# A two-layer graph network in float32: conv 2's node product in three float32r passes, b2 added by an accumulating transfer, and a new order of the work

## The chip, the cores and the metric

The kernel runs on one core of a Trainium2 chip. Its time is device time in microseconds (us), from the median of several runs; the runs shown for the kernel before are three. One execution of each kernel was also recorded by the hardware profiler, and its instructions are read below. The engines are named as in the profile: PE is TensorE (matmuls), PEld its weight loads, DVE is VectorE, ACT is ScalarE, POOL is GpSimd, and SP issues most of the transfers.

## The reference, cut to what matters

Each of 128 graphs g has 128 nodes with 512 features, x[g], and an adjacency matrix adj[g] of 128 x 128. All is float32.

```
h  = relu(layernorm(x))                        # over the 512 features
H  = (adj != 0);  w = adj[0, :]                # per graph
Be = 1 / columnsum(H);  Dn = 1 / (H w)
conv(z, W, b) = Dn * (H (Be * (H^T (z W^T)))) + b
h1 = layernorm(relu(conv(h, W1, b1))) * gamma + beta    # 1024 wide
x  = x + conv(h1, W2, b2) + h                           # back to 512
h2 = relu(layernorm(x))
agg = (adj h2) / max(rowsum(adj), 1e-6)
out = x + relu([h2, agg] W^T)
```

H Be H^T is one symmetric 128 x 128 matrix per graph, the node matrix S. Conv 1 applies S to the 512 features before W1; conv 2 applies W2 first (1024 to 512) and then S to the result: that last product is conv 2's node product.

## The kernel before

**Stages.** One graph is one unit of work: its 128 nodes lie on the 128 partitions. The function step(s) writes out by hand one pass of a software pipeline in which several graphs are in different stages: conv 1 of graph s, the normalisation and conv 2 of s-1, the node product of conv 2 and the first half of layer 1 of s-2, the weights and aggregation of layer 1 of s-3, the end of s-4, and preparations for s+1, s+2 and s+3. A stage is a small function with an argument g, decorated so that it runs once and only for graphs that exist. head() does graphs 0 to 2 together with the loading and splitting of the weights; tail() does the last graphs. The instructions of each engine run strictly in the order in which these functions emit them, and so do the transfers on each issuing queue (SP, ACT, POOL). The framework adds the waits between engines. No planner runs: the order in the source is the order on the chip.

**Exact products.** The large matmuls (lines 455 and 460) are made with float32r operands, which TensorE takes in one pass. To keep float32's accuracy each operand is split in two or three parts. ACT makes a high part (L537, L426), DVE or POOL subtracts it from the value for a low part (the helper combine, L80, or L430), and DVE makes a third combination of both (L546, L433). product() then runs three groups of matmuls: high by high and low by low into one bank of PSUM (names ending in m: rm, gm, bm, am) and the third into a second bank (rd, gd, bd, ad). ACT copies the first bank out with a factor just over one, and DVE adds the second. Only the small products are left as plain float32 matmuls: ps_s (the node matrix, L375), pz (conv 1's node product, L413) and py (conv 2's node product, L628).

**Around the change.** conv2_weights runs gm and gd; conv2_main (ACT, L615) and conv2_weights_out (DVE, L619) make G; conv2_bias adds c0, the share of beta, on POOL (L80, tile g); conv2_nodes multiplies S by G in float32 into py; conv2_out (DVE, L632) adds py times Dn to X. X itself was prepared by residual, in which POOL adds h and then b2 (broadcast to all partitions, b2_bc) to x. layer1_self_main and layer1_self_out (L704, L716) bring the last product out of PSUM, and finish (L721) applies relu, adds X and issues the store on SP. Small work sits on DVE: scales (L305, L306) turns a variance into the two numbers of a layernorm; mean_operator (L320 to L323) divides adj by its row sums; incidence (L361 to L369) makes H and H Be; node_scale (L386 to L389) makes Dn. inner_turn and layer1_turn (L516) are block transposes; their operands come through DRAM and back (n_scratch, h_scratch, an_scratch, L501 and L509).

**Buffers.** The main products rotate through six banks of PSUM, the small ones (ps_s, pz, py) through two. Many SBUF tiles share a tag and so a buffer: a tile can be written only when all readers of the one before it are done. In the last graphs, place() puts tiles into weight buffers that are no longer needed. fill(n) puts dummy matmuls of n columns ahead of the next bank.

Of the kernel before, what the change touches and what calls it, by code (L numbers as in the profile page):

```python
# [24 lines left out]
def gnn_kernel(  # L25
# [45 lines left out]
    pool = ctx.enter_context(tc.tile_pool(name="pool", bufs=1))  # L71
    dram = ctx.enter_context(tc.tile_pool(name="dram", bufs=3, space=DRAM))
# [9 lines left out]


# [118 lines left out]
    def unit():  # L202
        t = pool.tile([P, 3, P], FP, tag="anp", name="unit").bitcast(FR)
        zero = pool.tile([P, P], FP, tag="ant", name="zero")
        nc.gpsimd.memset(zero, 0.0)
        for i, v in enumerate((1.0, -1.0)):
            nc.gpsimd.affine_select(out=t[:, i], in_=zero, compare_op=ALU.not_equal, fill=v, base=0,
                                    pattern=[[-1, P]], channel_multiplier=1)
            UNIT.append(t[:, i])
# [49 lines left out]
    def beta_out():  # L259
        nc.vector.tensor_scalar(c0, BETA[0], DOWN_12, None, MUL)  # L260
# [28 lines left out]

    STATS = {}  # L290

    def sums(key, src, junk, width, func=AF.Identity):
        STATS[key] = t = pool.tile([P, 8], FP, tag=f"st{key[0]}", name="st", bufs=2)
# [9 lines left out]
    def scales(g, kind):  # L303
        t = STATS[kind, g]
        nc.vector.reciprocal(t[:, 4:5], t[:, 3:4])  # L305
        nc.vector.tensor_tensor(t[:, 5:6], t[:, 1:2], t[:, 4:5], MUL)  # L306
# [9 lines left out]
    def mean_operator(g):  # L316

        a = ADJ.pop(g)
        deg = pool.tile([P, 1], FP, tag="deg", name="deg", bufs=2)
# [3 lines left out]
        nc.vector.tensor_scalar(a, a, deg, None, MUL)  # L323
# [13 lines left out]
    def mean_transpose(g):  # L337
# [4 lines left out]
        parts = place(pool, [P, 3, P], "anp", "anp", g).bitcast(FR)  # L342
# [14 lines left out]
    def incidence(g):  # L357
# [4 lines left out]
        SB[g] = sb = pool.tile([P, P + 1], FP, tag="sb", name="sb")  # L362
        nc.vector.tensor_scalar(sb[:, P : P + 1], at[:, 0:1], DOWN_12, None, MUL)
        cnt = pool.tile([P, 1], FP, tag="cnt", name="cnt", bufs=3)
# [4 lines left out]
        nc.vector.tensor_scalar(sb[:, :P], at, cnt, None, MUL)  # L369
# [3 lines left out]
    def node_matrix(g):  # L373
        ps = small_bank("ps_s")
        nc.tensor.matmul(ps[:, : P + 1], HT.pop(g), SB.pop(g), start=True, stop=True)  # L375
        s = pool.tile([P, P + 1], FP, tag="s", name="s", bufs=4)
        copy(s, ps[:, : P + 1], AF.Copy)  # L377
# [4 lines left out]
    def node_scale(g):  # L382
        w = DN[g]
        DN[g] = dn = pool.tile([P, 3], FP, tag="dinv", name="dinv", bufs=6)
# [4 lines left out]
        nc.vector.tensor_scalar(dn[:, 1:2], dn[:, 0:1], ONE_UP, None, MUL)  # L389

# [14 lines left out]
    def residual(g, eng=nc.gpsimd):  # L405
        combine(eng, X[g], X[g], H0[g], ADD)
        combine(eng, X[g], X[g], b2_bc, ADD)
# [205 lines left out]
    def conv2_main(g):  # L613
        G[g] = t = place(pool, [P, D], "A", "g", g)
        copy(t, PY.pop(g), AF.Copy, scale=ONE_UP)  # L615

    @stage
    def conv2_weights_out(g):
        nc.vector.tensor_tensor(G[g], PG.pop(g), G[g], ADD)  # L619
# [4 lines left out]

    @stage
    def conv2_nodes(g):
        PY[g] = py = small_bank("py")
        nc.tensor.matmul(py, S.pop(g), G.pop(g), start=True, stop=True)  # L628

    @stage  # L630
    def conv2_out(g):
        nc.vector.scalar_tensor_tensor(X[g], PY.pop(g), DN.pop(g)[:, 0:1], X[g], MUL, ADD)  # L632
# [86 lines left out]
    def finish(g):  # L719
        o = OP.pop(g)[0]  # L720
        nc.vector.scalar_tensor_tensor(o, o, 0.0, X.pop(g), MAX, ADD)  # L721
        nc.sync.dma_start(out=out[g], in_=o)

    def step(s):
        layer1_self_main(s - 4)
        conv2_bias(s - 2)
        layer1_high(s - 3)  # L730
        x_norm(s + 1)
        node_matrix(s + 1)
        conv2_nodes(s - 2)
        layer1_self_out(s - 4)
        mean_out(s - 3)
        inner_out(s - 1)
        inner_in(s - 1)
        finish(s - 4)
        layer1_low(s - 3)
        load_x(s + 2)  # L740
        mean_in(s - 3)
        load_adjb(s + 3)
        conv1_main(s, 0)
        conv2_out(s - 2)
        conv1_nodes(s + 1)
        conv1_weights(s, 1)
        load_adj(s - 2)
        layer1_sums(s - 2)
        layer1_spread(s - 2)
        layer1_rest(s - 3)  # L750
        conv1_out(s, 0)
        conv1_main(s, 1)
        layer1_mean(s - 3)
        inner_turn(s - 1)
        scales(s - 2, 3)
        layer1_self(s - 3)
        conv1_high(s + 1)
        conv1_out(s, 1)
        residual(s + 1)
        inner_high(s - 1)  # L760
        layer1_norm(s - 2)
        layer1_mean_main(s - 3)
        conv1_low(s + 1)
        conv1_bias(s, 0)
        mean_transpose(s - 3)
        conv1_bias(s, 1)
        inner_low(s - 1)
        layer1_mean_out(s - 3)
        layer1_trip_out(s - 2)
        inner_sums(s)  # L770
        layer1_mean_high(s - 3)
        conv1_rest(s + 1)
        mean_operator(s - 2)
        node_scale(s + 1)
        inner_spread(s)
        scales(s, 2)
        inner_rest(s - 1)
        conv2_weights(s - 1)
        layer1_mean_low(s - 3)
        mean_rest(s - 3)  # L780
        layer1_mean_rest(s - 3)
        incidence(s + 2)
        aggregate(s - 3)
        conv1_weights(s + 1, 0)
        x_sums(s + 2)
        inner_norm(s)
        x_spread(s + 2)
        conv2_main(s - 1)
        layer1_trip_in(s - 2)
        conv2_weights_out(s - 1)  # L790
        layer1_turn(s - 2)
        scales(s + 2, 1)

    def head():
        load_adjb(0, nc.scalar)
        load_w1(0, 0)
        copy(eps_root, eps, AF.Sqrt)
        w1[0].high(0)
        load_x(0)
        load_w1(0, 1)  # L800
        w1[0].low(0)
        x_sums(0)
        x_spread(0)
        load_w1(1, 0)
        fill(2816)
        w1[0].high(1)
        scales(0, 1)
        load_x(1)
        incidence(0)
        w1[0].low(1)  # L810
        unit()
        load_adjb(1)
        x_norm(0)
        w1[0].rest(0, nc.vector)
        node_matrix(0)
        conv1_nodes(0)
        load_w1(1, 1)
        incidence(1)
        x_sums(1, "A")
        load_w2(0)  # L820
        w1[1].high(0)
        load_affine()
        x_spread(1)
        scales(1, 1)
        conv1_high(0)
        node_matrix(1)
        conv1_low(0)
        conv1_rest(0)
        w1[1].high(1)
        w1[1].low(0)  # L830
        w1[0].rest(1, nc.gpsimd)
# [481 lines left out]
```

## Time and profile before

| what | value |
|---|---|
| median of 3 runs | 2480.91 us (2480.42 to 2481.21) |
| the profiled execution | 2481.01 us, span 2478.9 us from its first to its last instruction |
| granted TensorE clock, mean over the span | 0.998 |
| busy PE / PEld / DVE / ACT / POOL | 2461.9 / 2005.7 / 2004.5 / 1940.0 / 1715.1 us |
| 0 to 75 us | PE busy 67.7, DVE 63.3, ACT 63.6, POOL 47.0 |
| 100 to 2419 us | PE busy 2319.0, DVE 1876.1, ACT 1824.6, POOL 1643.5 of 2319.0 |
| 2419 to 2479 us | PE busy 52.1, DVE 46.2, ACT 31.9, POOL 5.6 |

A line of a timeline has the start in us from the beginning of the span, the duration in us, the engine, the source line, the operation, the tile written and the tiles read, the shape, and how many like it are merged; in brackets stands the engine's idle time ahead of it and what ended it. A group line has total busy us and the mean ns of one. A line of waits has the total, the number and the longest in us. Records of one engine overlap: an instruction often starts before the record of the one ahead of it ends, so what an instruction costs on a busy engine is the distance from its start to the next start.

### The profile page before, as it was taken

To read this page: it belongs to the slowest core of one execution; us is meant where nothing else is said; L and a number is where in the kernel's file an instruction comes from. 1 tells how busy PE (TensorE), PEld (TensorE's weight loads), DVE (VectorE), ACT (ScalarE), POOL (GpSimd) and SP (SyncE) were. 2 spreads that over 40 slices of the span, in tenths; PEclk is the share of its full clock that TensorE was granted. 3 is DMA by queue.
4 is the path that set the end of the run, shared out by engine and by line. 5 is a ranking of instruction groups with operands and counts; after the bars stand their busy time and mean duration, and the time that the engine had idled before them with its cause. 6 is when DMAs were issued, how large, how long until landed. Compare 5 with 4: busy or idle time off the path is not lost.

```text
span 2478.9 us, 41066 instructions
## 1 busy us (share of the span) xinstructions
PE 2461.9 (99%) x11188; PEld 2005.7 (81%) x11188; DVE 2004.5 (81%) x4906; ACT 1940.0 (78%) x4125; POOL 1715.1 (69%) x2275
## 2 busy tenths in 40 slices
PE   8999999999999999999999999999999999999998
PEld 6788888888888888888888888888888888888886
DVE  8888888888878888888788888787888888888887
ACT  8878877787788778877887787778777877887775
POOL 6677767776777677767767776777677767776761
PEclk9999999999999999999999999999999999999999
DMA  7344344434443443344334433443444344334432
GB/s 186 120 129 122 119 129 126 125 120 129 130 123 119 129 132 122 117 131 129 122 121 130 128 122 124 129 126 121 129 127 123 121 129 129 121 120 129 132 112 93
DMA packets 408951, 311.35 MB, mean 126 GB/s; under 512 B 176656, under 2 KB 339984, under 8 KB 408720
## 3 DMA queue, kind: packets, MB, share of 16 engines
q1 hardware_dynamic: 407888, 308.66, 40.6%
q8 instruction: 88, 1.44, 0.3%
q14 instruction: 143, 1.17, 0.2%
q10 hardware_dynamic: 576, 0.07, 0.0%
q0 software_dynamic: 256, 0.01, 0.0%
HBM read 166.21 MB, written 142.34 MB: 124 GB/s over the span
## 4 chain that ended last, share of the span: by engine, by line
PE 97%; DVE 1%; ACT 1%; DMA 0%; issue 0%; ACTq 0%; POOL 0%; SPq 0%; DVEq 0%
PE rm L455 19%; PE gm L455 19%; PE gd L460 9%; PE am L455 9%; PE bm L455 9%; PE rd L460 9%; PE bd L460 5%; PE ad L460 5%; PE py L628 4%; PE pz L413 4%; PE am L710 2%; PE ad L710 1%; PE ps_s L375 1%; DMA adjb<-in_adj_dram 0%; ACT r L294 0%
## 5 line engine op out<-in xcount | busy, mean ns | idle before, releaser
L80 POOL TENSOR_TENSOR g<-g,c 128x256 f32<-128x256 f32 x246 | 178.2, 745 | 631.9 <-DVE g L619 631.9
L80 POOL TENSOR_TENSOR r<-r,b_bc 128x256 f32<-128x256 f32 x500 | 360.2, 739 | 53.0 <-DVE r L480 47.4
L80 POOL TENSOR_TENSOR nl<-nt,nh 128x256 fp32r<-128x256 f32 x488 | 345.4, 734 | 0.0
L80 POOL TENSOR_TENSOR x_t<-x_t,b_bc 128x256 f32<-128x256 f32 x256 | 240.9, 961 | 3.0 <-DMA b_bc<-in_b_dram 3.0
L80 POOL TENSOR_TENSOR hl<-ht,hh 128x256 fp32r<-128x256 f32 x248 | 231.2, 954 | 6.4 <-ACT hh L537 6.2
L704 ACT ACTIVATE o<-am 128x512 f32<-128x512 f32 x127 | 76.1, 599 | 203.4 <-PE am L710 203.4
L294 ACT ACTIVATE h<-x_t 128x512 f32<-128x512 f32 x255 | 159.1, 624 | 96.6 <-DVE x_t L632 96.5
L480 DVE SCALAR_TENSOR_TENSOR r<-rd,dinv,r 128x512 f32<-128x512 f32 x256 | 190.6, 744 | 20.1 <-PE rd L460 7.3
L310 ACT ACTIVATE h<-x_t,st 128x512 f32<-128x512 f32 x255 | 204.7, 803 | 0.0
L683 DVE TENSOR_TENSOR gb_t<-bd,gb_t 128x512 f32<-128x512 f32 x127 | 87.9, 692 | 137.2 <-ACT gb_t L679 134.5
L80 POOL TENSOR_TENSOR x_t<-x_t,h 128x256 f32<-128x256 f32 x256 | 185.6, 744 | 5.6 <-ACT h L310 5.5
L632 DVE SCALAR_TENSOR_TENSOR x_t<-py,dinv,x_t 128x512 f32<-128x512 f32 x128 | 96.1, 751 | 115.3 <-PE py L628 115.3
L299 ACT ACTIVATE h<-x_t,st 128x512 f32<-128x512 f32 x255 | 182.7, 717 | 4.2
L413 PEld LDWEIGHTS pz<-s,h 128*128 128x128 f32 x1024 | 134.6, 192 | 60.1 <-ACT s L377 41.9
L475 ACT ACTIVATE r<-rm,dinv 128x512 f32<-128x512 f32 x256 | 173.2, 677 | 12.0 <-PE rm L455 11.7
L80 POOL TENSOR_TENSOR bl<-gb_t,bh 128x256 fp32r<-128x256 f32 x246 | 177.2, 739 | 1.8 <-PE am L455 1.8
L619 DVE TENSOR_TENSOR g<-gd,g 128x512 f32<-128x512 f32 x127 | 87.8, 692 | 92.3 <-PE gd L460 89.8
L310 ACT ACTIVATE r<-r,st 128x1024 f32<-128x1024 f32 x128 | 157.6, 1231 | 1.2 <-DVE st L306 1.2
L516 DVE STREAM_TRANSPOSE nt<-nb 128x1024 f32<-128x1024 f32 x127 | 156.3, 1230 | 1.6 <-DMA nb<-n_scratch 0.8
L721 DVE SCALAR_TENSOR_TENSOR o<-o,x_t 128x512 f32<-128x512 f32 x127 | 152.1, 1198 | 4.2
L546 DVE SCALAR_TENSOR_TENSOR nd<-nh,nl 128x1024 fp32r<-128x1024 f32 x127 | 155.2, 1222 | 0.0
L455 PE MATMUL rm<-w11h,z 128*128 128x512 f32 x512 | 151.3, 417 | 0.0
(217 smaller groups left out, 7242.3 us busy)
## 6 DMA issues: line engine op xcount, KB each, us to landing
n_scratch<-r SPq DMA_DIRECT2D x128, 512.0 KB, 2.6
nb<-n_scratch SPq DMA_DIRECT2D x508, 128.0 KB, 2.8
x_t<-in_x_dram SPq DMA_DIRECT2D x128, 256.0 KB, 2.9
h_scratch<-h SPq DMA_DIRECT2D x127, 256.0 KB, 2.0
hb<-h_scratch SPq DMA_DIRECT2D x508, 64.0 KB, 2.0
out_dram<-o SPq DMA_DIRECT2D x127, 256.0 KB, 2.2
adj_t<-in_adj_dram SPq DMA_DIRECT2D x128, 64.0 KB, 1.9
an_scratch<-adj_t SPq DMA_DIRECT2D x128, 64.0 KB, 1.7
```

The source lines that it names most:

```text
L80: eng.tensor_tensor(dst[:, s], a[:, s], b[:, s], op)
L294: copy(junk, src, func, accum_out=t[:, 0:1])
L299: copy(junk, src, AF.Square, bias=t[:, 1:2], accum_out=t[:, 2:3])
L310: copy(dst, src, func, bias=t[:, 5:6], scale=t[:, 4:5])
L413: nc.tensor.matmul(z[:, k * P : (k + 1) * P], H0[g][:, k * P : (k + 1) * P], S[g], start=True, stop=True)
L455: nc.tensor.matmul(pm, left[i](k), right(i, k), start=(i == 0 and k == 0), stop=(i == 1 and k == kk - 1))
L460: nc.tensor.matmul(pd, left[2](k), right(2, k), start=(k == 0), stop=(k == kk - 1), skip_group_check=True)
L475: copy(R[g][:, HALVES[half]], PY.pop((g, half)), AF.Copy, scale=DN[g][:, 1:2])
L480: nc.vector.scalar_tensor_tensor(r, PR.pop((g, half)), dn[:, 0:1], r, MUL, ADD)
L516: nc.vector.transpose(nt.rearrange("p k (i b) -> p k i b", b=B), t.rearrange("p i k a -> p k i a"))
L546: nc.vector.scalar_tensor_tensor(t, h, 2.0**-12, low, MUL, SUB)
L721: nc.vector.scalar_tensor_tensor(o, o, 0.0, X.pop(g), MAX, ADD)
```

## The change

Groups 3 to 120 are called steady; for them

- conv 2's node product becomes three float32r matmuls. S (now scaled by 4096) is split in three by node_high (ACT) and node_rest (two DVE operations), G in three by conv2_high (ACT), conv2_low (DVE) and conv2_rest (DVE). Two matmuls go to a bank ym, one to yd, both from the six main banks; conv2_out becomes two DVE operations, one for each bank.
- residual adds b2 by a transfer from b2_bc into X that accumulates, issued on POOL.
- finish leaves the store to a stage of its own, store, later on SP's queue.

For all groups

- conv2_main and conv2_weights_out carry a factor 4096 into G.
- scales keeps the reciprocal alone; the product goes to a stage shifts, on POOL or ACT or DVE as each call says. mean_operator leaves its scaling to mean_scale (ACT in the step), and incidence its last scaling to incidence_scale (POOL in the step).
- In the step, layer1_low, inner_low and layer1_mean_low go from POOL to DVE.
- Some tiles move to other pools (small, left).
- step, head and tail have a new order; head's fill of 2,816 columns becomes two of 128, and the tail gets one of 512.

Its core, with the whole new step (of head and tail, whose order changes throughout, the start of head):

```diff
+    FIRST, LAST = 3, N - 8
+
+    def steady(g):
+        return FIRST <= g <= LAST
+
+    def moved(t, src):
+        nc.gpsimd.dma_start(out=t, in_=src, accum_op=ADD)
...
+    def scaled(eng, dst, src, c):
+        if eng is nc.scalar:
+            copy(dst, src, AF.Copy, scale=c)
+        else:
+            eng.tensor_scalar(dst, src, c, None, MUL)
...
-        nc.vector.tensor_tensor(t[:, 5:6], t[:, 1:2], t[:, 4:5], MUL)
+
+    @stage
+    def shifts(g, kind, eng):
+        t = STATS[kind, g]
+        scaled(eng, t[:, 5:6], t[:, 1:2], t[:, 4:5])
...
-        nc.vector.tensor_scalar(a, a, deg, None, MUL)
+        ADJ[g] = a, deg
+
+    @stage
+    def mean_scale(g, eng):
+        a, deg = ADJ[g]
+        scaled(eng, a, a, deg)
...
-        nc.vector.tensor_scalar(sb[:, :P], at, cnt, None, MUL)
+        SB[g] = sb, cnt
+
+    @stage
+    def incidence_scale(g, eng):
+        SB[g], cnt = SB[g]
+        scaled(eng, SB[g][:, :P], HT[g], cnt)
...
-        copy(s, ps[:, : P + 1], AF.Copy)
+        copy(s, ps[:, : P + 1], AF.Copy, scale=4096.0 if steady(g) else 1.0)
...
-        combine(eng, X[g], X[g], b2_bc, ADD)
+        if steady(g):
+            moved(X[g], b2_bc)
+        else:
+            combine(eng, X[g], X[g], b2_bc, ADD)
...
+    @stage
+    def conv2_high(g):
+        if steady(g):
+            GP[g] = t = left.tile([P, 2, D], FP, tag="t3", name="gp").bitcast(FR)
+            copy(t[:, 0], G[g], AF.Copy, scale=DOWN)
+
+    @stage
+    def conv2_low(g, eng=nc.gpsimd):
+        if steady(g):
+            combine(eng, GP[g][:, 1], G.pop(g), GP[g][:, 0], SUB)
+
+    @stage
+    def node_high(g):
+        if steady(g):
+            SP[g] = t = left.tile([P, 8, P], FP, tag="t1", name="sp").bitcast(FR)
+            copy(t[:, 0], S[g], AF.Copy, scale=DOWN / 4096.0)
+
+    @stage
+    def node_rest(g):
+        if steady(g):
+            t, full = SP[g], S.pop(g)
+            nc.vector.scalar_tensor_tensor(t[:, 1], t[:, 0], -4096.0, full, MUL, ADD)
+            nc.vector.scalar_tensor_tensor(t[:, 2], t[:, 0], -4097.0, full, MUL, ADD)
+
+    @stage
+    def conv2_rest(g):
+        if steady(g):
+            t = SP[g].rearrange("p k c -> p (k c)")[:, D : 2 * D]
+            h, l = GP[g][:, 0], GP[g][:, 1]
+            nc.vector.scalar_tensor_tensor(t, h, DOWN_12, l, MUL, SUB)
+            GP[g] = h, l, t
...
+        pm, pd = bank("ym"), bank("yd")
+        parts, (h, l, d) = SP.pop(g), GP.pop(g)
+        nc.tensor.matmul(pm, parts[:, 0], h, start=True, stop=False)
+        nc.tensor.matmul(pm, parts[:, 1], l, start=False, stop=True)
+        nc.tensor.matmul(pd, parts[:, 2], d, start=True, stop=True)
+        PY[g] = pm, pd
...
+        for p, c in zip(PY.pop(g), (1, 0)):
+            nc.vector.scalar_tensor_tensor(X[g], p, dn[:, c : c + 1], X[g], MUL, ADD)
...
     def step(s):
+        node_high(s - 2)
+        layer1_high(s - 3)
         conv2_bias(s - 2)
+        inner_out(s - 1)
+        inner_in(s - 1)
+        conv2_high(s - 2)
+        node_rest(s - 2)
+        node_matrix(s + 1)
+        mean_out(s - 3)
+        layer1_low(s - 3, nc.vector)
+        layer1_self_main(s - 4)
+        conv1_weights(s, 1)
+        mean_in(s - 3)
+        conv2_low(s - 2, nc.vector)
+        layer1_self_out(s - 4)
+        conv2_rest(s - 2)
+        conv2_nodes(s - 2)
+        finish(s - 4)
+        load_adj(s - 2)
+        layer1_rest(s - 3)
+        x_norm(s + 1)
+        conv1_main(s, 0)
+        conv2_out(s - 2)
+        store(s - 4)
+        conv1_nodes(s + 1)
+        conv1_main(s, 1)
+        conv1_out(s, 1)
+        conv1_out(s, 0)
+        conv1_high(s + 1)
+        conv1_bias(s, 1)
+        layer1_mean(s - 3)
+        inner_turn(s - 1)
+        layer1_sums(s - 2)
+        conv1_bias(s, 0)
+        conv1_low(s + 1)
+        layer1_self(s - 3)
+        layer1_mean_main(s - 3)
+        layer1_spread(s - 2)
+        load_adjb(s + 3)
+        inner_high(s - 1)
+        scales(s - 2, 3)
+        mean_transpose(s - 3)
+        shifts(s - 2, 3, nc.gpsimd)
+        layer1_norm(s - 2)
+        inner_sums(s)
+        layer1_mean_out(s - 3)
+        layer1_mean_high(s - 3)
+        inner_low(s - 1, nc.vector)
+        mean_rest(s - 3)
+        inner_rest(s - 1)
+        layer1_mean_low(s - 3, nc.vector)
+        layer1_mean_rest(s - 3)
+        inner_spread(s)
+        scales(s, 2)
+        shifts(s, 2, nc.gpsimd)
+        conv2_weights(s - 1)
+        layer1_trip_out(s - 2)
+        residual(s + 1)
+        incidence(s + 2)
+        inner_norm(s)
+        aggregate(s - 3)
+        node_scale(s + 1)
+        load_x(s + 2)
+        mean_operator(s - 2)
+        conv2_main(s - 1)
+        layer1_trip_in(s - 2)
+        conv2_weights_out(s - 1)
+        x_sums(s + 2)
+        x_spread(s + 2)
+        mean_scale(s - 2, nc.scalar)
+        conv1_rest(s + 1)
+        layer1_turn(s - 2)
+        incidence_scale(s + 2, nc.gpsimd)
+        conv1_weights(s + 1, 0)
+        scales(s + 2, 1)
+        shifts(s + 2, 1, nc.vector)
...
     def head():
+        load_w1(0, 0)
+        load_x(0)
         load_adjb(0, nc.scalar)
-        load_w1(0, 0)
         copy(eps_root, eps, AF.Sqrt)
         w1[0].high(0)
-        load_x(0)
-        load_w1(0, 1)
         w1[0].low(0)
-        x_sums(0)
-        x_spread(0)
-        load_w1(1, 0)
-        fill(2816)
```

## The prediction

> **What bounds the kernel now.** I read the busy shares first, then one step of the steady state as a timeline of TensorE and VectorE, then the list of waits.
>
> ```profile
> PE 2461.9 (99%) x11188; PEld 2005.7 (81%) x11188; DVE 2004.5 (81%) x4906; ACT 1940.0 (78%) x4125; POOL 1715.1 (69%) x2275
> ...
> PE 97%; DVE 1%; ACT 1%; DMA 0%; issue 0%; ACTq 0%; POOL 0%; SPq 0%; DVEq 0%
> ...
> POOL g L80 <- DVE g L619: 631.9, 123, 5.3
> ...
> DVE x_t L632 <- PE py L628: 115.3, 123, 1.2
> ```
>
> TensorE is busy 99% and is 97% of the chain that ended last. Such a share alone can deceive, since matmuls overlap; the starts settle it. In the steady state the same group of matmuls starts every 19.013 to 19.034 us, mean 19.018, and in them no matmul waits: here its own queue of matmuls is the time. One step of it:
>
> ```profile
> 1209.85 1.07 PE L460 MATMUL rd<-w10d,z 128*128 128x512 f32 x4
> 1210.76 0.38 PE L375 MATMUL ps_s<-sb,adjt 128*128 128x129 f32 x2
> 1210.97 1.02 PE L628 MATMUL py<-g,s 128*128 128x512 f32 x2
> 1211.84 1.05 PE L413 MATMUL pz<-s,h 128*128 128x128 f32 x8
> 1212.64 1.18 PE L455 MATMUL rm<-w11h,z 128*128 128x512 f32 x4
> 1213.67 1.08 PE L455 MATMUL rm<-w11l,z 128*128 128x512 f32 x4
> ```
>
> What counts is from start to start. Four float32r matmuls of 512 columns take 0.907 us (0.227 each). The fp32 product of conv 2 (py, two records) takes 0.860, though its two records of 594 ns add up to 1.188. The first group after the fp32 pz takes 1.013: 0.11 too long, and the next 0.01. The other engines have room: in the 19 us from 119 to 138, DVE was busy 15.3, ACT 15.0, POOL 13.5 us.
>
> **TensorE's part of the change.** py's 0.860 goes; three float32r matmuls come (ym, ym, yd). Their nearest rows are the three of the aggregation (L710), which start 0.229, 0.232 and 0.227 apart: 0.688. The order becomes ps_s, rm11 (12 matmuls), ym, ym, yd, pz, bm. So a float32r group now follows ps_s too: in the head a ps_s followed at once by such groups makes 2.07 us with the next two of them (37.92 to 39.99), which is 0.256 above 2 x 0.907, where ps_s cost 0.220. pz keeps its price and the 0.1 behind it (the trace's last pz, after a float32r group, has the same 0.81). Sum: 0.860 - 0.688 - 0.036 = about 0.15 us a step, 19.018 to 18.864. Groups 3 to 120, 118 of them, use the new form: 118 x 0.154 = 18.2 us.
>
> Here a rule can be weighed. Rows: 0.860 for fp32, 0.688 for three passes. The Trainium skill counts four passes for true fp32 (FP8 and Floating Point Precision, TensorE Precision Notes) and 512/2.4 + 2.5 = 216 ns for an isolated warm pass (TensorE: Matmul & The Clock Gate, Back-to-back issue gap): 0.864 against 0.648, which would give 0.216 x 118 = 25 us. fp32 agrees, but this trace's passes start 0.227 to 0.232 apart, so I take 18.2.
>
> **VectorE's part: the cover is almost used up.** This decides. In the step 1199.46 to 1218.49 DVE waited 3.39 us: 1.13 before gb_t, 0.14 and 0.22 at two st lines, 0.85 before g, 1.05 before x_t (L632), each the start less the time at which it could have started. It was occupied 15.64, by starts; a 512-wide operation takes 0.60 though its record has 0.69, a 1024-wide one 1.14. Of this some is contention with POOL:
>
> ```profile
> 1204.70 0.68 DVE L546 SCALAR_TENSOR_TENSOR bd<-bh,bl 128x512 fp32r<-128x512 f32 x1
> ...
> 1209.83 1.24 DVE L721 SCALAR_TENSOR_TENSOR o<-o,x_t 128x512 f32<-128x512 f32 x1
> ...
> 1212.70 0.88 DVE L546 SCALAR_TENSOR_TENSOR hd<-hh,hl 128x512 fp32r<-128x512 f32 x1
> ...
> 1209.78 1.87 POOL L80 TENSOR_TENSOR hl<-ht,hh 128x256 fp32r<-128x256 f32 x2
> ```
>
> The three DVE lines are of one size with both tensors in SBUF; bd ran while POOL was idle, the others beside it. Excess: 0.56 for finish, 0.21 for hd, 0.26 for the scaling of adj_t (L323), 0.18 for the small dinv line (L388): 1.21. Without it DVE needs 14.43.
>
> Added, by starts: the second conv2_out 0.67 plus 0.12, because the second waits for the first's result; conv2_low 0.60; node_rest 2 x 0.20 (L347); conv2_rest 0.60; and from POOL hl 0.60, nl 1.14, bl 0.73 (bd waits for it at once): 4.86. Taken away: two small shifts 0.16, the scalings of adj_t and sb 0.20 each, and 0.12 because something now stands between self_out and finish: 0.68. So 14.43 + 4.86 - 0.68 = 18.61 us, against TensorE's 18.86.
>
> How much contention stays? Laying DVE's new order end to end from node_rest as 0: hl to hd are at 0.4 to 4.0, nl to bd at 9.6 to 13.7. POOL now has the g bias (after g, 17.2 to 18.7), four r additions (6.3 to 9.2), two shifts, x+h (14.0 to 15.4), its transfer and the sb scaling. Only node_rest (0.1) and dinv (0.18) can meet it: 18.7 to 18.9. A rule of the skill speaks against the change: the pair of ports that VectorE shares with GpSimd is a lock, and a two-input DVE operation and a POOL operation that reads SBUF block each other until the first is done (SBUF — State Buffer, Who interferes with whom). By it each of the two meetings could cost a whole POOL addition, 0.74, so 20.1 us; in the rows hd lost 0.21 and finish 0.56 with POOL busy throughout. I go by the rows, 18.75: TensorE still sets the step, with 0.1 us to spare.
>
> Do waits fit in? Behind a late DVE wait stand ym's readers, then r and z, for which TensorE waits. With ym starting at t, x_t (at 4.0) needs ym by about t + 0.75, so t at most 3.26; rd10 needs z (ready 17.84) at t + 15.0, so t at least 2.85. ym's bank is am's of the step before, free when ACT has copied o (about 1.5). bm, bd, agg and gd have 0.8 us or more. The other loop is g, g bias on POOL, conv2_high on ACT, conv2_low: low is ready at 0.83 and wanted at 1.0. ACT gets 0.9 us (adj_t, node_high, conv2_high) and keeps about 2.4 idle; POOL falls from 13.5 to about 8. Both cost nothing under TensorE, and without that cover their delay goes straight to conv2_low, DVE's next wait.
>
> **The transfer.** POOL gives up 1.9 us of b2 additions and gets the issue of an accumulating DMA, 128 rows of 2 KB. No row shows one. Nearest:
>
> ```profile
> L241 POOL DMA_DIRECT2D gb<-in_beta_dram x4 | 2.4, 597 | 0.2 <-issue 0.2
> ```
>
> That is 32 rows; below, 0.55; above, four times it by rows, 2.2. DMA: Bandwidth & Descriptors (Latency and other measured facts) gives about 1 us from issue to first byte on GpSimd's path. I take 1.1, between the row and four rows' worth, nearer to the page since the row's descriptors are far smaller. Queued behind it on POOL are the sb scaling (L232: 1.57 us for 512 columns, so about 0.5) and the next g bias. The loop from st through POOL's shift, x+h, transfer, sb, bias, high and low back to st is 17.2 us plus this issue. At 1.1 it is 18.3 and hidden. Landing is not urgent: X is next read three steps later.
>
> SP still issues 22 transfers a step at about 0.43, 9.5 us. store and adjb now come last, h_scratch, x, hb, n, nb, an, anb, adj before. Latest is hb, held until bl frees its buffer (13.1): landed near 16.9, ht wants it at 17.7. anb lands near 7.2, wanted at 8.7; nb has 3 us. So nothing.
>
> **Head and tail.** Fill of 2,816 columns falls to two of 128 (and 512 in the tail). It ran from 0.9 to 7.5 us, before the first real matmul at 10.3, so dropping it saves nothing by itself; the granted clock was half from 10.2 to 17.0 anyway. Colder start, earlier x and adjacency, moved beta rows and splits: no row prices these. The first 100 us hold 9.1 us without matmuls and the last 60 hold 8.0, and a 1.8 us wait for nd at 80 brought another 3.4 us at half clock. From this I allow 6 us gain to 5 us loss, and take 0 as the two ends nearly cancel.
>
> **Sum.** Span 2478.9 - 18.2 = 2460.7; around it lie 2.1 (2481.0 profiled), so 2462.8. The profiled time is 0.1 over the median of 2480.9. Forecast: 2463.
>
> **Rivals.** (1) Half given away: DVE's 18.75 is 0.15 to 0.25 too low, since 0.1 us margins are rarely kept by three in-order engines. Steps of 18.9 to 19.0: 2467 to 2479. For it: every margin above is below 0.3; against: the rows repeat to a few ns. (2) Slower: POOL's issue takes over 1.65 us. Then 17.2 + issue is the step; from 1.8 us on it exceeds the old one. At 2.0 the step is 19.2: 118 x 0.18 = 21 us slower, 2502. For it: four times the rows of the nearest line, and 2 KB in each instead of 32 bytes; against: that line's 0.55 leaves room for three times as much. (3) No gain in TensorE: by record durations, 2 x 594 = 1188 against 3 x 394 = 1182, or bank waits before ym eat it: 2480. Against: the starts. (4) Head gain on top: 2452 to 2457.
>
> **How the numbers follow.** TensorE-bound as worked out: 0.60, 2457 to 2469 with head and tail. Half given away: 0.14, half of it below 2476. Slower by POOL or DVE: 0.18. No gain: 0.03. Head gain: 0.05. Time 2463. About 0.2% (5 us) is what a measurement can tell. Faster: 0.60 + 0.05 + 0.07 = 0.72; same: 0.07 + 0.03 = 0.10; slower 0.18. The range takes the first, the head gain's near half, rival 1 and the milder part of rival 2, leaving out about 0.03 below and 0.15 above: 2454 to 2488.
>
> **What would show it.** Group starts 18.86 apart with TensorE without idle; ym, ym, yd 0.69; DVE near 18 busy of 18.9 with finish back at about 0.69 and hd at 0.68; POOL's issue about 1.1. Wrong if TensorE waits each step for conv2_low, conv2_rest or z, if finish stays near 1.2, or if the issue is over 1.65.

## The result and the profile after

| | before | after |
|---|---|---|
| median | 2481.06 us (2480.42 to 2481.32, 4 runs) | 2458.68 us (2458.32 to 2458.89, 4 runs) |
| span of the profiled execution | 2478.9 us | 2457.1 us |
| steady step, from start to start of the same group of matmuls | 19.018 us | 18.860 us |

The ratio is 0.991, with a 95% interval of 0.9893 to 0.9927. The forecast was 2463, with a range of 2454 to 2488.

First the page of the profile after: busy times of the engines, the shares of the chain that ended last, and the new transfer among the issues (count, size of one, median us from issue to landing).

```profile
PE 2437.2 (99%) x11300; PEld 2023.8 (82%) x11300; DVE 2340.8 (95%) x5358; ACT 2061.8 (84%) x4494; POOL 1016.1 (41%) x1560
...
PE 83%; DVE 12%; issue 2%; ACT 2%; DMA 1%; SPq 0%; POOL 0%; DVEq 0%; ACTq 0%; POOLq 0%
...
x_t<-b_bc POOLq DMA_DIRECT2D x118, 256.0 KB, 3.7
```

TensorE is busy as before, in 24.7 us less. VectorE went from 81% to 95%, POOL from 69% to 41%. The chain now passes through VectorE for 12%, yet the list of waits has only one matmul of a steady step (yd, once, for 0.2 us). VectorE's wait for py, now a matter of the groups that are not steady alone, stands in it with (total, number and longest, in us)

```profile
DVE x_t L710 <- PE py L697: 6.9, 7, 2.0
```

Before, it stood at 115.3 us. In the same 19 us as in the prediction (columns: busy time and instructions of PE, PEld, DVE, ACT, POOL, then granted clock, DMA share, GB/s):

```profile
119.00:138.00 19.00, 19.00 (x91) 15.86 (x90) 18.23 (x45) 16.30 (x37) 7.86 (x13) 1.00 0.52 141
```

VectorE is busy 18.23 instead of 15.3, POOL 7.86 instead of 13.5. One step of TensorE, as a timeline:

```profile
1216.42 0.38 PE L404 MATMUL ps_s<-sb,adjt 128*128 128x129 f32 x2
1216.56 1.18 PE L489 MATMUL rm<-w11h,z 128*128 128x512 f32 x4
1217.57 1.08 PE L489 MATMUL rm<-w11l,z 128*128 128x512 f32 x4
1218.49 1.08 PE L494 MATMUL rd<-w11d,z 128*128 128x512 f32 x4
1219.41 0.39 PE L701 MATMUL ym<-gp,sp 128*128 128x512 f32 x1
1219.64 0.39 PE L702 MATMUL ym<-gp,sp 128*128 128x512 f32 x1
1219.86 0.39 PE L703 MATMUL yd<-sp 128*128 128x512 f32 x1
1220.09 1.05 PE L447 MATMUL pz<-s,h 128*128 128x128 f32 x8
1220.90 1.17 PE L489 MATMUL bm<-w30h,hh 128*128 128x512 f32 x4
1221.90 1.07 PE L489 MATMUL bm<-w30l,hl 128*128 128x512 f32 x4
```

The three passes stand at 1219.41, 1219.64 and 1219.86, pz at 1220.09: 0.68 us where py took 0.86. The operations of VectorE that the prediction had called contended, and one that it had not weighed fully:

```profile
1215.77 0.51 DVE L682 SCALAR_TENSOR_TENSOR sp<-sp,s 128x128 fp32r<-128x128 f32 x1
1216.20 0.28 DVE L683 SCALAR_TENSOR_TENSOR sp<-sp,s 128x128 fp32r<-128x128 f32 x1
...
1218.84 0.69 DVE L803 SCALAR_TENSOR_TENSOR o<-o,x_t 128x512 f32<-128x512 f32 x1
1219.45 0.68 DVE L580 SCALAR_TENSOR_TENSOR hd<-hh,hl 128x512 fp32r<-128x512 f32 x1
```

finish fell from 1.24 to 0.69 and hd from 0.88 to 0.68. The first of node_rest's two equal operations takes 0.51 against the second's 0.28: POOL's bias on g runs beside it.

**Where the 21.8 us of span come from.** The fourth product gm starts at 94.41 us instead of 98.86: 4.45. From there to the last gm it is 2335.34 instead of 2352.69: 17.35. Behind the last gm nothing changes (27.35 against 27.34). The 17.35 are 118 x 0.158 = 18.6 for the steady groups, less 1.2 for six steps that are longer than 18.860 (the longest 19.373); five of the six are told of in the last section.

### The profile page after: what moved, and what is told of

The parts are those of the page before. It is cut to its first block, busy times and chain, and to the rows that moved or that the text cites. A ratio compares the mean times of both kernels' runs of the same rounds, so it can differ in the third digit from the quotient of the medians.

```text
span 2457.1 us, 41143 instructions
## 1 busy us (share of the span) xinstructions
PE 2437.2 (99%) x11300; PEld 2023.8 (82%) x11300; DVE 2340.8 (95%) x5358; ACT 2061.8 (84%) x4494; POOL 1016.1 (41%) x1560
## 3 DMA queue, kind: packets, MB, share of 16 engines
q14 instruction: 142, 1.16, 0.2%
## 4 chain that ended last, share of the span: by engine, by line
PE 83%; DVE 12%; issue 2%; ACT 2%; DMA 1%; SPq 0%; POOL 0%; DVEq 0%; ACTq 0%; POOLq 0%
PE gm L489 16%; PE rm L489 16%; PE bm L489 8%; PE am L489 8%; PE gd L494 8%; PE rd L494 8%; PE bd L494 4%; PE ad L494 4%; PE pz L447 4%; PE am L791 2%; PE ad L791 1%; DVE r L514 1%; PE ps_s L404 1%; PE yd L703 1%; PE ym L701 1%
## 5 line engine op out<-in xcount | busy, mean ns | idle before, releaser
L303 POOL TENSOR_SCALAR st<-st 128x1 f32<-128x1 f32 x252 | 76.1, 302 | 566.9 <-DVE st L320 566.9
L460 ACT ACTIVATE z<-pz 128x512 fp32r<-128x512 f32 x128 | 76.5, 598 | 206.3 <-PE pz L447 206.3
L81 POOL TENSOR_TENSOR g<-g,c 128x256 f32<-128x256 f32 x246 | 211.1, 1019 | 3.8 <-DVE g L653 3.8
L81 DVE TENSOR_TENSOR nl<-nt,nh 128x1024 fp32r<-128x1024 f32 x126 | 152.2, 1208 | 0.0
L489 PE MATMUL bm<-w30h,hh 128*128 128x512 f32 x504 | 146.9, 413 | 0.1
L314 ACT ACTIVATE junk<-r,st 128x1024 bf16<-128x1024 f32 x128 | 145.1, 1134 | 0.1
L489 PE MATMUL rm<-w11l,z 128*128 128x512 f32 x512 | 138.2, 392 | 0.0
L494 PE MATMUL rd<-w11d,z 128*128 128x512 f32 x512 | 138.0, 391 | 0.0
L447 PE MATMUL pz<-s,h 128*128 128x128 f32 x1024 | 135.9, 276 | 1.9 <-ACT s L406 1.3
L489 PE MATMUL rm<-w10h,z 128*128 128x512 f32 x512 | 137.7, 391 | 0.0
```

Source lines behind the costliest of these rows:

```text
L81: eng.tensor_tensor(dst[:, s], a[:, s], b[:, s], op)
L314: copy(junk, src, AF.Square, bias=t[:, 1:2], accum_out=t[:, 2:3])
L447: nc.tensor.matmul(z[:, k * P : (k + 1) * P], H0[g][:, k * P : (k + 1) * P], S[g], start=True, stop=True)
L460: copy(h, pz, AF.Copy, scale=DOWN)
L489: nc.tensor.matmul(pm, left[i](k), right(i, k), start=(i == 0 and k == 0), stop=(i == 1 and k == kk - 1))
L494: nc.tensor.matmul(pd, left[2](k), right(2, k), start=(k == 0), stop=(k == kk - 1), skip_group_check=True)
```

## The experiments

The theory was: TensorE's own queue sets the step; the three passes shorten it by 0.158 us; the dealing-out and the new order only make room so that nothing waits; VectorE has little to spare. The rivals: the new order or the dealing-out brings the time by itself; VectorE is the bound; the transfer matters. Every edit below is to the kernel after the change unless another is named. "Step" is the distance of equal groups in the steady part.

### conv 2's node product in fp32 again

```diff
-        copy(s, ps[:, : P + 1], AF.Copy, scale=4096.0 if steady(g) else 1.0)
+        copy(s, ps[:, : P + 1], AF.Copy, scale=1.0)
...
     def conv2_nodes(g):
-        if not steady(g):
+        if True:
             PY[g] = py = small_bank("py")
```

The split stages and conv2_out turn to their fp32 form by the same condition.

> The new order, the dealing-out, the transfer, the head and the tail stay; conv 2's node product alone is one fp32 matmul again for every graph, and the five split stages and the second addition to x go. Theory (TensorE's own queue sets the step, and the three passes save 0.158 us of it): a steady step of 19.018 us again, 118 x 0.158 = 18.6 us more, about 2477 us. Rival (the gain comes from the new order and the dealing-out, the product is by the way): about 2459 us, unchanged.

Measured: 2481.75 us (1.0002 of the time before, 0.9994 to 1.001), steps of 19.046 to 19.093, mean 19.06. The whole gain is gone, though order, dealing-out, transfer, head and tail are all still the new ones. 3.0 us of the head's gain are still there (the fourth gm starts at 95.82 us), but the steps use them up: they are 0.04 us longer than the 19.018 that the expectation took, so that the time is 4.7 us over the 2477 expected. So the rival falls: without the three passes the rest is worth nothing in the steps, and even a little less than nothing. In the old order ps_s, py and pz followed one another, here ps_s stands apart, and TensorE changes from fp32 to float32r twice instead of once; by starts, ps_s with the three groups behind it takes 2.99 us, where ps_s and three such groups took 2.94.

### The third pass left out

```diff
-        pm, pd = bank("ym"), bank("yd")
+        pm = bank("ym")
...
-        nc.tensor.matmul(pd, parts[:, 2], d, start=True, stop=True)
-        PY[g] = pm, pd
+        PY[g] = pm, pm
```

> The third pass of the node product (the matmul into yd) is left out, so a part of the product is missing; VectorE still makes its operand and still adds twice to x, both times from ym. TensorE's step becomes 18.860 - 0.227 = 18.633 us. If TensorE alone sets the step, the time falls by 118 x 0.227 = 26.8 us, to about 2432 us. If VectorE is fully used at 18.86 us (the prediction left it 0.1 us), the step falls by 0.1 us at most: 2447 to 2459 us.

Measured: 2433.18 us, steps of 18.633, as TensorE's queue alone has it; 25.5 us less. TensorE sets the step, and VectorE keeps up at 18.63 with all its operations still there. Only the second addition to x starts 0.78 us behind the first here and not 0.86, which leaves VectorE 0.08 us less. So it has at least 0.15 us to spare at 18.86, not 0.1. One pass costs 0.227 us.

### One small operation more on VectorE

```diff
             nc.vector.scalar_tensor_tensor(d, h, -4097.0, full, MUL, ADD)
+            nc.vector.scalar_tensor_tensor(d, h, -4097.0, full, MUL, ADD)
```

> One of the two 128x128 operations that split the mean operator is written twice on VectorE (the same result twice, nothing reads it in between): 0.20 us more on VectorE in each step by the starts in the trace, nothing more on TensorE. If VectorE has at most 0.1 us to spare, the step grows by 0.1 to 0.2 us: 2470 to 2482 us. If it has 0.2 us or more to spare: about 2459 us.

Measured: 2469.35 us; most steps 18.87 to 18.93. This lies just below the first expectation, but the added size was wrong: the second operation writes what the first wrote and starts 0.32 us behind it instead of 0.20, so that nd starts 0.33 us later than without it. 18.893 less 0.33 leaves 18.56 us for VectorE's own need.

### One 512-column operation more on VectorE

```diff
             nc.vector.scalar_tensor_tensor(d, h, ONE_UP, pz, MUL, SUB)
+            nc.vector.scalar_tensor_tensor(d, h, ONE_UP, pz, MUL, SUB)
```

> The last part of conv 1's left operand (z from h and pz, 128x512) is made twice on VectorE, the same result twice: 0.60 us more on VectorE in each step by its starts in the trace. With this much VectorE sets the step, and the step less 0.60 us is what VectorE itself needs: 18.75 us as the prediction took it gives steps of 19.35 us and 118 x 0.49 = 58 us more (2517 us); 18.67 us, read from the steps of 18.89 us with 0.20 us added, gives 19.27 us and 48 us more (2507 us); 18.63 us or less gives at most 44 us more (2503 us).

Measured: 2505.71 us, steps of 19.20. Again the repetition cost more than its size, 0.71 us by starts. 19.20 less 0.71 is 18.49; here node_rest no longer met POOL's bias and took 0.16 us less, which gives 18.65 with it. This run and the one before it put VectorE's need at about 18.55 to 18.65 us, and its room under TensorE at 0.2 to 0.3 us, which the run without the third pass allows. In the trace after the change this room is hard to see, because records of VectorE overlap by some 0.07 us and swallow short waits. It shows where starts are compared with the run above: from st to ant 0.178 us against 0.064, from z to st 0.593 against 0.576, from gp to o 0.633 against 0.602, and so on, 0.2 us in all.

### ps_s next to pz

```diff
-        node_matrix(s + 1)
         mean_out(s - 3)
...
         store(s - 4)
+        node_matrix(s + 2)
         conv1_nodes(s + 1)
...
-        incidence(s + 2)
+        incidence(s + 3)
```

(load_adjb and incidence_scale likewise one graph earlier, and incidence(5) with its scale at the end of head.)

> The node matrix's fp32 matmul (ps_s) is put directly ahead of conv 1's fp32 node product (pz), with the incidence work made one graph earlier, so that a step changes from fp32 to float32r once instead of twice. The trace shows about 0.11 us of delay after each change (rm11h after ps_s 1.018 against 0.907 us). If TensorE sets the step and this delay belongs to the change of type, the step falls by 0.11 us: 118 x 0.11 = 13 us, about 2446 us. If VectorE is at its limit too, little or nothing of it comes out: 2452 to 2459 us. If the delay belongs to the length of ps_s and not to the change of type: 2459 us, and the delay stands after pz with 0.2 us.

Measured: 2465.76 us, slower than all three expectations, and steps of 18.840 to 18.848, mean about 18.846: 0.014 less, not 0.11. The timeline of TensorE in this kernel:

```profile
1224.49 0.38 PE L404 MATMUL ps_s<-sb,adjt 128*128 128x129 f32 x2
1224.71 1.06 PE L447 MATMUL pz<-s,h 128*128 128x128 f32 x8
1225.52 1.18 PE L489 MATMUL bm<-w30h,hh 128*128 128x512 f32 x4
1226.54 1.08 PE L489 MATMUL bm<-w30l,hl 128*128 128x512 f32 x4
```

Ahead of pz, ps_s takes 0.22 to the next start; ahead of a float32r group it took 0.14 and the groups behind it 0.13 more. So most of the "delay after a change of type" was ps_s's own work, shown one row later. A change costs about 0.04 to 0.05 us, near the 0.036 of the prediction, and here 0.036 of the 0.050 saved comes back in the groups behind pz. The higher total has another place: from the second gm to the third and from there to the fourth it is 22.70 and 19.67 us instead of 17.84 and 19.19, because the earlier incidence work was squeezed into the end of head (at 72.4 us TensorE waits 4.07 us there for the scaling of sb on POOL), and the first tail steps take 19.65. The saving of 118 x 0.014 = 1.7 us doesn't pay for that.

### b2 by two POOL additions instead of the transfer

```diff
         combine(eng, X[g], X[g], H0[g], ADD)
-        if steady(g):
+        if False:
             moved(X[g], b2_bc)
```

> b2 is added to x by two POOL additions of 256 columns in the steady steps too, as before the change; everything else stays. POOL is held some 1.5 us (two of about 0.74 us) instead of the 0.66 us from the transfer's issue to the next start, so 0.8 us more between VectorE's release of the shift and conv 2's bias. By the prediction's working (held up to 1.65 us is hidden) the time stays at 2459 us. If the trace's tighter placing counts (g's bias ends at 1216.1 us, VectorE takes its low part at 1217.0 us), VectorE's low part waits some 0.6 us, and with 0.2 us to spare there the step grows by about 0.4 us: 2500 to 2515 us. In between if only the contention with VectorE counts (0.1 to 0.2 us on VectorE): 2459 to 2470 us.

Measured: 2458.03 us (2457.19 to 2458.51), steps of 18.860: no difference to the kernel after the change that counts (0.65 us less, and it lacks the longer steps, which come to about as much). So the transfer has no part in the gain. The second expectation is refuted. POOL in the kernel after the change, as a timeline:

```profile
1211.42 1.43 POOL L81 TENSOR_TENSOR x_t<-x_t,h 128x256 f32<-128x256 f32 x2
1213.15 0.90 POOL L91 DMA_DIRECT2D x_t<-b_bc  x1 [0.30 <-DVE dinv L418]
1213.81 0.91 POOL L303 TENSOR_SCALAR sb<-adjt,cnt 128x128 f32<-128x128 f32 x1
1214.39 1.73 POOL L81 TENSOR_TENSOR g<-g,c 128x256 f32<-128x256 f32 x2
```

and with the two additions:

```profile
1211.86 1.43 POOL L81 TENSOR_TENSOR x_t<-x_t,h 128x256 f32<-128x256 f32 x2
1213.25 1.44 POOL L81 TENSOR_TENSOR x_t<-x_t,b_bc 128x256 f32<-128x256 f32 x2
1214.67 0.63 POOL L303 TENSOR_SCALAR sb<-adjt,cnt 128x128 f32<-128x128 f32 x1
1215.26 1.44 POOL L81 TENSOR_TENSOR g<-g,c 128x256 f32<-128x256 f32 x2
```

From the start of x+h to the end of g's bias it is 4.70 us with the transfer and 4.84 with the additions. sb's scaling starts 0.96 us after the end of x+h with the transfer (0.30 before its start, 0.66 to the next), and 1.38 with the additions; but behind the transfer the records of sb's scaling and of g's bias end 0.29 us later (0.91 instead of 0.63, 1.73 instead of 1.44). What is left is 0.14 us, and nothing in this kernel wanted it.

### The residual moved to where VectorE does long operations

```diff
         shifts(s - 2, 3, nc.gpsimd)
+        residual(s + 1)
         layer1_norm(s - 2)
...
         layer1_trip_out(s - 2)
-        residual(s + 1)
```

> The residual (x plus h on POOL, and the transfer that adds b2) is moved to the place right behind layer 1's shift, where POOL was idle and VectorE does its long operations nl, nd, bl and bd; POOL's way to conv 2's bias loses some 2 us. If the transfer's issue waits for VectorE's short operations (in the trace it starts 0.30 us after x plus h ends, and three times over 1 us late, with VectorE named as the releaser): it starts only some 2 to 3 us after x plus h ends. If it waits for nothing on VectorE: within 0.1 us. The time stays at 2459 us as long as TensorE sets the step; VectorE has 0.2 to 0.3 us to spare, and a contention above that shows as a longer step: 0.2 us over it is 24 us, 2483 us.

Measured: 2556.14 us, steps of 19.63, far above the 2483 expected. The transfer's question has a plain answer: it starts 0.30 us after x+h ends, and the profile now names POOL's own x+h as what released it. It doesn't wait for VectorE; the name in the trace above (dinv) was a coincidence. The time is the find. VectorE and POOL in this kernel:

```profile
1212.62 1.81 DVE L81 TENSOR_TENSOR nl<-nt,nh 128x1024 fp32r<-128x1024 f32 x1
1214.36 0.82 DVE L371 SCALAR_TENSOR_TENSOR anp<-anp,ant 128x128 fp32r<-128x128 f32 x1
...
1212.62 0.73 POOL L81 TENSOR_TENSOR x_t<-x_t,h 128x256 f32<-128x256 f32 x1
...
1213.32 1.72 POOL L81 TENSOR_TENSOR x_t<-x_t,h 128x256 f32<-128x256 f32 x1
```

x+h now meets nl and anp, operations with two inputs from SBUF, and the two engines take turns. POOL's first addition starts with nl and takes its usual 0.73 us; nl takes 1.81 instead of 1.21 and ends 1.08 us after that addition. POOL's second addition takes 1.72 and ends 0.60 us after nl; the first anp takes 0.82 instead of 0.28 and ends 0.15 us after that. The rows of before show the same. There POOL's additions beside finish (1209.83, 1.24 us) and hd (1212.70, 0.88 us) were

```profile
1209.78 0.74 POOL L80 TENSOR_TENSOR hl<-ht,hh 128x256 fp32r<-128x256 f32 x1
...
1212.31 0.73 POOL L80 TENSOR_TENSOR x_t<-x_t,h 128x256 f32<-128x256 f32 x1
```

and finish and hd each end 0.55 us after theirs. In eight of the kernels here (before, after, and the six that change POOL's work) the medians agree: a VectorE operation with two inputs from SBUF that starts more than 0.01 us into one of POOL's additions ends a fixed time after it, 0.55 us with 512 columns, 1.08 with 1024, 0.15 to 0.16 with 128 and 0.02 with one. So it waits for the addition to end, and what it loses is what was left of the addition at its start, less about 0.13 us. With an input from PSUM there is no such loss: r takes 0.74 us and conv2_out 0.75 with POOL adding or not.

VectorE loses 1.14 us and gets some 0.25 back at node_rest and dinv, which x+h and the bias no longer meet. Less the 0.2 to 0.3 us to spare this makes 0.6 to 0.7; the step grows by 0.77, and TensorE waits for z (the largest gap, behind rm's low group, is 0.63 us above its 0.907). So the place of the residual, where it meets a single operation of this kind, the small dinv, is what the new order gets right.

### The low parts back on POOL: all three, layer 1's alone, the inner one alone

```diff
-        layer1_low(s - 3, nc.vector)
+        layer1_low(s - 3)
...
-        inner_low(s - 1, nc.vector)
+        inner_low(s - 1)
...
-        layer1_mean_low(s - 3, nc.vector)
+        layer1_mean_low(s - 3)
```

> The three low parts that the change dealt to VectorE (inner, layer 1 and mean product) go back to POOL in the steady steps, in the new order: VectorE is relieved of about 2.5 us, POOL gets eight additions of about 0.74 us (6 us more). If TensorE's own queue sets the step and the dealing-out is only room that was not needed: 2459 us, steps of 18.860 us, with longer two-operand operations on VectorE. If POOL's chain from r's bias over nl and bl to the next residual then comes late: 1 us or more in a step, 2480 to 2570 us.

> Of the three low parts only layer 1's (hl, 128x512) goes back to POOL, behind conv 2's bias, two additions of 0.74 us; VectorE is relieved of 0.60 us. POOL is idle there for 6.3 us, and hd, the next reader, comes 3 us after VectorE's hl in the trace. If only chains that wait count: steps of 18.860 us, 2459 us. If any low part on POOL costs by contention what VectorE has to spare: 0.1 us or more in a step, 2470 us or more.

> Of the three low parts only the inner one (nl, 128x1024) goes back to POOL, four additions of 0.74 us behind r's bias; VectorE is relieved of 1.13 us. POOL would end nl near 1209.5 us of the trace instead of VectorE's 1207.9 us, and VectorE's nd, next in its queue but for two short ones, waits for it. If this chain is what costs 1.53 us a step with all three on POOL: steps of 19.8 to 20.4 us, 2570 to 2652 us. If the cost lay in the other two: 2459 us.

| low parts on POOL | median | step |
|---|---|---|
| none (after the change) | 2458.68 | 18.860 |
| layer 1's | 2461.05 | 18.860 |
| the inner one | 2602.64 | 20.02 |
| all three | 2652.37 | 20.39 |

The inner one costs 1.16 us of the 1.53, as expected; all three together lie above the 2570 us that were the most expected. The waits of the kernel with it alone on POOL (total, number, longest; from 300 to 2100 us, some 90 steps), and then VectorE's second anp operation and nd in its timeline:

```profile
DVE nd L580 <- POOL nl L81: 118.5, 89, 1.3
...
PE rd L494 <- DVE z L467: 58.8, 90, 1.0
```

```profile
1217.54 0.82 DVE L372 SCALAR_TENSOR_TENSOR anp<-anp,ant 128x128 fp32r<-128x128 f32 x1
1219.70 1.22 DVE L580 SCALAR_TENSOR_TENSOR nd<-nh,nl 128x1024 fp32r<-128x1024 f32 x1 [1.33 <-POOL nl L81]
```

VectorE is relieved of 1.13 us of work and given 1.33 us of waiting. Besides, its two anp operations now meet POOL's additions for nl and take 0.87 and 0.82 us instead of 0.28 each, 1.13 us more. Less the 0.2 to 0.3 us to spare this is about the 1.16 measured, and what VectorE makes later (z) comes late for TensorE. Layer 1's low part changes no steady step; its 2.4 us are seven longer steps (up to 20.13, together 3.2 us above 18.860 where the kernel after the change has 0.8 us of such), told of in the last section. So the move of the inner low part was needed, that of layer 1's was not. The mean product's was not tried alone; with all three on POOL, VectorE's bd waits 0.66 us a step for it.

### The three passes alone, in the order before the change

The kernel before the change, with the split stages of the diff, and in its step

```diff
+        node_high(s - 2)
...
+        conv2_high(s - 2)
+        node_rest(s - 2)
...
-        conv2_nodes(s - 2)
...
+        conv2_low(s - 2, nc.vector)
         finish(s - 4)
+        conv2_rest(s - 2)
...
-        conv2_out(s - 2)
-        conv1_nodes(s + 1)
         conv1_weights(s, 1)
+        conv2_nodes(s - 2)
+        conv2_out(s - 2)
+        conv1_nodes(s + 1)
```

> The kernel before the change with the split of conv 2's node product alone: its parts, three passes and second addition to x, placed where the old order lets them (the product behind conv 1's second half, conv 1's node product behind it, as in the new order). POOL keeps its 13.5 us of work, with the low parts and b2's additions; nothing is dealt out anew, and VectorE gets about 2.7 us more. If the three passes are all that counts and the dealing-out is not needed: steps of 18.86 us, about 2462 us. If POOL's share makes VectorE late (as with the three low parts on POOL, where steps took 20.39 us): steps over 19.02 us, slower than before the change, 2490 to 2660 us.

Measured: 2804.51 us, 1.131 of the time before and more than the 2660 that were the most expected; steps between 20.8 and 22.8 us, most of them near 21.1 or 22.7. TensorE waits about 1.8 us a step for nd (up to 2.0). The steps near 22.7 are those in which the granted clock falls as well: it is 0.92 or 0.93 in the mean over such a step and 1.00 over the others. finish is back at 1.23 us and conv2_rest is at 1.22 instead of 0.68, both beside POOL's additions, and ACT's first pass over x for layer 1 waits 4.0 us a step for conv2_out. So in these places TensorE's saving of 0.16 is lost many times over for want of room on the other engines. It is one placement only; that no better one exists in the old order isn't shown.

### The old head

head() of the kernel before, with the new small stages right behind those that they came out of.

> The head before the change, with its fill of 2816 columns and its order, ahead of the new steps and tail (the new small stages stand right behind the ones they came out of, on VectorE). If the 4.4 us by which the fourth conv 2 product starts earlier in the head come from the head's order: about 2463 us, steps of 18.860 us, and in its trace the wait for nd near 80 us and a stretch at half clock after it, as before the change. If they come from elsewhere (the way into the first steps): about 2459 us.

Measured: 2460.86 us, steps of 18.860, no wait for nd and no half clock near 80 us. Busy times of the same two stretches (columns as above) before the change, and then with the old head ahead of the new steps:

```profile
80.00:82.00 2.00, 0.26 (x1) 0.26 (x2) 2.00 (x4) 1.97 (x5) 0.53 (x1) 1.00 0.18 36
82.00:86.00 4.00, 4.00 (x12) 3.12 (x12) 2.65 (x10) 1.72 (x5) 0.43 (x1) 0.59 0.57 197
```

```profile
80.00:82.00 2.00, 2.00 (x10) 1.65 (x10) 1.75 (x10) 1.38 (x3) 1.57 (x3) 1.00 0.42 109
82.00:86.00 4.00, 4.00 (x21) 3.32 (x20) 3.10 (x7) 3.77 (x12) 3.09 (x5) 1.00 0.78 214
```

Before the change TensorE did 13 matmuls in these 6 us, with the clock at 0.59 in the second stretch; the new first step does 31. The third gm is 19.06 us ahead of the fourth here, 19.19 after the change, 22.91 before it; with the product in fp32 again it is 19.21, so the three passes have no part in it. So the 3.7 us lay in the way in which the old order took its first step, and the head's own order is worth 1 to 2 us (2.2 between the medians, 1.0 between the profiled spans; the start of the first gm varies from 43.5 to 45.7 us among the kernels that share the new head).

## Why the prediction was right, and where it was not

- **TensorE sets the step, 19.018 to 18.864.** Right: 18.860, and leaving out one pass takes exactly its 0.227. The terms, by starts: the three passes take 0.682 (taken 0.688; the saving is 0.178, not 0.172); ps_s ahead of float32r costs 0.050 more (taken 0.036; the head's row had the rest in its third group, 39.99 to 40.91, which was not counted); pz with the group behind it costs 0.021 less, and the aggregation 0.007 less (both taken as unchanged). Sum 0.156, against 0.158 measured. The 216 ns that the Trainium skill gives for an isolated matmul (TensorE: Matmul & The Clock Gate, Back-to-back issue gap), from which the estimate of 25 us came, is not met here: a float32r pass behind another takes 0.227 us, as the run without the third one shows by its step.
- **VectorE at 18.75 us, 0.1 to spare.** It fits under TensorE's step, as forecast, and needs 18.55 to 18.65. That the figure came so near is in part luck, for its terms were off in both directions. Too small were the contention (0.14 taken; beside POOL node_rest's pair takes 0.64 us instead of 0.49, and dinv 0.39 instead of 0.16), node_rest itself (0.40 taken, 0.49), the second conv2_out (0.08 more than taken) and bl (0.07 more). Too small as well was what the dealing-out frees: where the shift or the scaling is gone, the reciprocal ahead of it costs VectorE 0.06 to 0.11 us to the next start instead of 0.15 to 0.20, which makes some 0.4 us in the four places. Rival 1 (half given away) rested on the margin and did not come about.
- **Contention by the rows, not by the lock.** The reading of the rows was wrong, and the place of POOL's work saved the forecast. The traces show the lock of the Trainium skill (SBUF — State Buffer, Who interferes with whom): the one that comes second waits until the first is done. The rows that were set against it are such waits. POOL's addition had 0.69 us left when finish started and 0.33 when hd did, and less 0.13 these are the 0.56 and 0.21. In the new order 0.35 us is left when node_rest starts and 0.37 when dinv does, so the rule makes about 0.45 us of the two meetings (an estimate from these figures), not two whole additions. The first of node_rest lost 0.23 and dinv 0.23; finish and hd met nothing and came back to 0.68. The moved residual shows nearly the full price, 0.60 and 0.54 us.
- **The transfer's issue, 1.1 us and hidden.** Hidden it is, and the additions would have been too. From the end of x+h to the next start it is 0.96 us, and 1.25 with the later ends behind it, so 1.1 was a fair size; the time from issue to first byte, on which it leant, no run here shows. Rival 2 needed over 1.65 and was not met; where it would have decided was not tried. sb's scaling (0.91, taken 0.5) and the shift (0.30, taken 0.2) were under-sized, without effect.
- **SP's transfers: no cost.** Right: the one matmul of a steady step that waits (yd) does so behind a late issue on POOL, told of in the last section.
- **Head and tail at nothing.** This is the term that was mis-sized, and most of the 4.3 us between forecast and result. The 1.8 us wait for nd and the 3.4 us at half clock behind it were seen and put among the things that might come or go. They belonged to the first step's order, which the change rewrote, and both vanished: 3.7 us. Rival 4 (a head gain on top) had 6 to 11 us there; with the 0.7 us from ahead of the third gm it was 4.45. The tail did change nothing.
- **No gain in TensorE (rival 3).** Refuted by the starts and by the fp32 run.

## What to carry to other kernels

When the bounding engine's queue is shortened, the price lies on the others: measure their room by adding a known operation or shortening the bound, since overlapping records hide short waits and a busy share of 95% can still have 1 to 2% to give. Where POOL adds two SBUF tensors matters more than how many such additions there are: a VectorE operation with two inputs from SBUF that starts in the middle of one waits for its end (0.23 us at dinv, 0.54 to 0.60 at the moved residual), so put the additions beside transposes and reads of PSUM, which lost nothing here. A small loss in the rows can be the tail of a long wait: see what was left of the other engine's operation at the start. A wait with a clock drop behind it in the first pass through a rewritten loop belongs in the sum of the change, not in the noise of the head.

## What was not expected of the hardware

- With the transfer in place three of the 118 issues start 1.0 to 1.6 us after x+h instead of 0.30 (at 1100.7, 2044.3 and 2101.0 us), and the node_rest operation of VectorE that then meets POOL's bias takes 1.21, 1.79 and 0.96 us instead of 0.5, as it waits for the second of the bias's two additions (it ends 0.16 us after it). With POOL additions none is above 0.67. The late issues are the same three of the 118 (the 56th, 106th and 109th) in every kernel here that has the transfer. With layer 1's low part on POOL, node_rest then takes 2.6 to 2.9 us: there POOL has more additions standing behind the late one. Most of the longer steps are these. What delays the issue is open.
- Behind the transfer POOL's next operations end 0.29 us later each (sb's scaling, g's bias), though their starts follow one another as without it. Why was not tested.
- Writing the same tile twice in a row costs VectorE 0.11 to 0.13 us over the operation itself (0.33 for 0.20, 0.71 for 0.60).
